# Six exponential buffers instead of three in the attention layers of a four-layer graph network

## The chip, the cores and the metric

The kernel runs on one core of a Trainium2 chip. The metric is the device time of one execution in microseconds (us), the lower the better. Before the change it is 3087.09 us, the median of three runs (3085.15, 3087.09 and 3092.65 us).

## What is computed

The input is x (3327 nodes, 256 features each) and adj (3327 x 3327, about 1% of it positive, with a positive diagonal). Four layers follow one another. Each normalises x row by row, takes the positive part, and adds the layer's result to x. Layer 0 is a top-p attention with two propagation steps. Layer 1 filters the adjacency with a tanh and multiplies it with a projection of the nodes. Layers 2 and 3 are graph attention; the change touches layers 1, 2 and 3. Cut to what matters:

```python
# layer 1
filt = tanh(adj * adj) * (adj > 0)            # the 700 largest of a row are kept
x = x + relu(filt @ (tanh(h @ W_proj + b_proj) @ W_gcn) + b_gcn)
# layers 2 and 3 (layer 2 also masks in the diagonal; layer 3 ends with elu)
Wh = h @ W
e = leaky_relu((Wh @ a[:256])[:, None] + (Wh @ a[256:])[None, :], 0.2)
alpha = softmax(where(adj > 0, e, NEG_INF), axis=1)
x = x + alpha @ Wh
```

## The kernel before

Everything is one core's program. It is written with tiles and pools; a planner in the framework then fixes, while the program is built, in which order each engine's instructions stand, and puts in the waits. Each engine works through its own list in that order, so an instruction that waits holds up everything behind it on its engine. Tiles that share a slot of memory (`slot(tag, ...)`) wait for the last use of the tile that was there.

The nodes are padded to 26 row tiles of 128. Layers 2 and 3 are two calls of `attention` (L1546 on). It takes the row tiles in seven spans: six of four tiles and a last one of two. For one span it walks over the 26 column tiles two at a time; such a step of two column tiles is called a pair here, and a span has 13 of them. What one pair costs on each engine:

- ScalarE (ACT) writes four exponentials: twice the first one, L1615, `e1 = exp(s0 + sd)`, and twice the second one, L1616, `e2 = exp(s1 + d2)` (512 elements per partition each with four tiles in the span). The larger of the two is the exponential of the leaky relu.
- VectorE (DVE) takes their maximum into e1 (L1617) and masks it with the stored signs of adj (L1618), both over 1024 elements.
- TensorE (PE) multiplies the eight blocks of e1 with Wh (L1624), 257 columns wide: 128 features in two halves and the denominator.

The places for e1 and e2 are handed out in turn by a counter:

```python
e1, e2 = exps[count[1] % 3][:, :n], exps2[count[1] % 2][:, :n]
```

Three places of e1 lie in slot e0, one place of e2 in slot e4 and one in slot e5. A place of e1 is free again when PE has multiplied it, a place of e2 when the maximum has read it.

A softmax needs a bound on each row's scores for the next span. For each of its row tiles (four, or two for the last span) DVE runs over a whole mask row, L1631 (128 x 3327, the largest dk among a row's neighbours), in the steps b = 1 to 4 of the span before; `junk` is where it writes the products that nobody reads. Then `scores_of` (L1551 on) makes small vectors of the bounds (L1554 to L1565), PE spreads them over the partitions (L1571), ACT copies them to `sb` (L1574), and ACT sets up the next `top` from `sb` (L1586), into which the next span's L1631 writes. At a span's end the denominators are inverted (L1649) and the results finished: in layer 2 with L1670, in layer 3 with L1676 to L1681 and an output DMA.

Under layer 2 the entry of layer 3 is prepared for every row tile that is finished: statistics on DVE (L131, L132), three small steps on GpSimd (POOL; L794, L795, L1414), `turned` (ACT L1420 writes hr, PE transposes it at L786, ACT copies it to ht at L787), `projected` (PE L1428, ACT L1432 and L1433), and for a whole span `spread` (PE L1445, ACT L1448, and DVE L1452 four times). These pieces are put on a list, `todo`, and one entry of it is taken per step b from 1 on.

Layer 1 (L1490 on) takes the row tiles one by one. For each it loads two halves of a column of blocks into one of three double places (two in slots e4 and e5, a third one in the pool `l1`), filters them (DVE L1501, ACT L1502), multiplies (PE L1505), and then, a few tiles behind, sums (L1483), turns and projects the entry of layer 2. It also makes the byte masks `pos` that L1631 reads (L1523) and stores them. The pool `att`, with four buffers of signs and masks, takes the memory that pool `l1` held.

Of the kernel before, what the change touches and what calls it, by code (L numbers as in the profile page):

```python
# [20 lines left out]
P = 128  # L21
N = 3327
NT = 26
# [43 lines left out]
def kernel(  # L67
# [679 lines left out]
    def layers(fast):  # L747
# [21 lines left out]
        def slot(tag, shape, name, dtype=F32):  # L769
            return big.tile(shape, dtype, tag=tag, name=name)  # L770
# [703 lines left out]
        places = [slot(f"e{4 + n}", [P, 2, HB * P], f"blk1_{n}") for n in range(2)]  # L1474
        entry2 = Entry("2", w2l, nodes(("a0", "a1"), D + 2, "wh2"), "bl", True)
        with tc.tile_pool(name="l1", bufs=2, reuse_waits="tile") as l1:
            third = l1.tile([P, 2, HB * P], F32, bufs=1, name="blk1_2")
            places = [[places[n][:, k, :] for n in range(2)] for k in range(2)] + [[third[:, n, :] for n in range(2)]]
            po_of = {}

            def summed(it):
                pre = late.tile([P, D], F32, tag="fin_a", bufs=2, name="pre")
                nc.vector.tensor_tensor(pre, po_of.pop(it), bg, ALU.add)  # L1483
                nc.vector.scalar_tensor_tensor(xn(it), pre, 0.0, xs(it), ALU.max, ALU.add)
                entry2.stats(it, xn(it))

            def projected(it):
                entry2.projected(it)
                if it in ends:
                    entry2.spread(ends.index(it))  # L1490

            for it in range(NT):
                if it % 2 == 0:
                    po2 = ps_wide()
                po = po_of[it] = po2[:, 512 * (it % 2) : 512 * (it % 2) + D]
                for hb in range(2):
                    filt = places[it % 3][hb]
                    nc.sync.dma_start(
                        filt, adj_t[it, :, hb * HB : (hb + 1) * HB, :].rearrange("p j i -> p (j i)")
                    )  # L1500
                    nc.vector.scalar_tensor_tensor(filt, filt, 0.0, filt, ALU.max, ALU.mult)  # L1501
                    nc.scalar.activation(filt, filt, AF.Tanh)  # L1502
                    for j in range(HB):
                        jc = hb * HB + j
                        nc.tensor.matmul(  # L1505
                            po, filt[:, j * P : (j + 1) * P], gw(jc), start=(jc == 0), stop=(jc == NT - 1)
                        )
                if it >= 1:
                    summed(it - 1)
                if it >= 2:  # L1510
                    entry2.turned(it - 2, xn(it - 2))
                if it == 2:
                    entry2.shifted()
                if it >= 3:
                    projected(it - 3)
                ar = slot(f"e{it % 2}", [P, NP], "adj_rows")
                r = rows_of(it)
                if r < P:
                    nc.vector.memset(ar, 0.0)
                for a, b in rows_to_load(it):  # L1520
                    nc.sync.dma_start(ar[a:b, :N], adj[it * P + a : it * P + b, :])
                pos = pos_first[:, it, :] if it in spans[0] else l1.tile([P, NP], U8, tag="pos", name="pos")
                nc.vector.tensor_scalar(  # L1523
                    pos[:, :N], ar[:, :N], 0.0, None, ALU.is_gt, ALU.add, accum_out=counts[:, it : it + 1]
                )
                nc.gpsimd.memset(pos[:, N:], 0)
                nc.sync.dma_start(pos_d[it], pos)
            summed(NT - 1)
            projected(NT - 3)
            entry2.turned(NT - 2, xn(NT - 2))  # L1530
            projected(NT - 2)
            entry2.turned(NT - 1, xn(NT - 1))
            projected(NT - 1)


        att = fast.enter_context(tc.tile_pool(name="att", bufs=1, reuse_waits="tile"))
        e0, e4, e5 = (slot(f"e{k}", [P, NP], f"places{k}") for k in (0, 4, 5))

        exps = [e0[:, 1024 * k : 1024 * (k + 1)] for k in range(3)]
        exps2 = [t[:, :1024] for t in (e4, e5)]  # L1540
        exps, exps2 = ([t.rearrange("p (t j i) -> p t j i", t=4, j=2) for t in ts] for ts in (exps, exps2))
        sbs = [e5[:, 1024 * k : 1024 * (k + 1)].rearrange("p (q m) -> p q m", q=2) for k in (1, 2)]
        junk = e4[:, 1024 : 1024 + NP // 2].bitcast(BF16)
        count = [0, 0]

        def attention(entry, finish, following=None):  # L1546
# [33 lines left out]
            for i, span in enumerate(spans):  # L1580
# [16 lines left out]
                for b, j0 in enumerate(range(0, NT, JB)):  # L1597
# [8 lines left out]
                    for j in range(0, nj, 2):  # L1606
                        jc = j0 + j
                        for q in range(2):
                            if eye and jc + q in span:
                                own = signs[:, jc + q - span[0], j + q, :]  # L1610
                                nc.vector.tensor_tensor(own, own, ident, ALU.max)
                        e1, e2 = exps[count[1] % 3][:, :n], exps2[count[1] % 2][:, :n]
                        count[1] += 1
                        for q in range(2):
                            nc.scalar.activation(e1[:, :, q, :], s0, AF.Exp, bias=sd[:, jc + q, 1:2])  # L1615
# [20 lines left out]
                            sb_next = scores_of(ahead, top)  # L1636
                    if following is not None and (i, b) == (1, 1):
                        following.shifted()
                    if b and todo:
                        for work in todo.pop(0):  # L1640
                            work()
                for k, it in enumerate(span):
                    if not eye:
# [30 lines left out]
        def finish3(it, po, rden):  # L1674
# [7 lines left out]
            for a, b in rows_to_load(it):  # L1682
                nc.sync.dma_start(out[it * P + a : it * P + b, :], o[a:b, :])

        attention(entry3, finish3)


# [82 lines left out]
```

## Time and profile before

| | |
|---|---|
| median of three runs | 3087.09 us |
| the profiled execution | 3088.28 us |
| its span, first to last instruction | 3086.4 us |
| PE busy in the span | 2806.9 us (91%) |
| DVE busy | 2405.2 us (78%) |
| ACT busy | 1932.0 us (63%) |
| last multiplication of layer 1 starts before | 2329.7 us |
| first multiplication of layer 2 | 2357.2 us |
| first multiplication of layer 3 | 2747.9 us |
| last multiplication of layer 3 | 3075.8 us |

The profile records one execution. Times on its axis run from the start of the span; the 1.9 us that the execution has over the span lie around it. L with a number is a line of the kernel. A row of a group gives the count, the busy time and the mean of one; a row of the waits gives who waited for whom, the total, the number of times and the longest; a row of a window gives the length and, for each engine, its busy time in the window. Matmuls overlap in PE, so that a PE that shows as busy may still start work late: what counts is the distance from one start to the next.

### The profile page before, as it was taken

To read this page: it belongs to the slowest core of one execution; us is meant where nothing else is said; L and a number is where in the kernel's file an instruction comes from. 1 tells how busy PE (TensorE), PEld (TensorE's weight loads), DVE (VectorE), ACT (ScalarE), POOL (GpSimd) and SP (SyncE) were. 2 spreads that over 40 slices of the span, in tenths; PEclk is the share of its full clock that TensorE was granted. 3 is DMA by queue.
4 is the path that set the end of the run, shared out by engine and by line. 5 is a ranking of instruction groups with operands and counts; after the bars stand their busy time and mean duration, and the time that the engine had idled before them with its cause. 6 is when DMAs were issued, how large, how long until landed. Compare 5 with 4: busy or idle time off the path is not lost.

```text
span 3086.4 us, 37597 instructions
## 1 busy us (share of the span) xinstructions
PE 2806.9 (91%) x13350; PEld 2274.9 (74%) x13350; DVE 2405.2 (78%) x4145; ACT 1932.0 (63%) x2583; POOL 433.7 (14%) x768
## 2 busy tenths in 40 slices
PE   7789999999999978989999988999997999979998
PEld 5467777777778756767777767888886777868887
DVE  3988688678678289998888679577766999779996
ACT  5777677678675347666677466433334667767776
POOL 0100000000001033111111115211120333210000
PEclk9889999999999999999999999999998999989999
DMA  4302312312332252222223332378870211112221
GB/s 124 95 12 76 97 48 73 97 58 68 94 98 77 79 152 78 64 59 78 75 59 92 92 111 66 136 297 324 332 254 25 65 58 57 32 49 79 76 75 36
DMA packets 186779, 302.24 MB, mean 98 GB/s; under 512 B 25116, under 2 KB 140759, under 8 KB 183255
## 3 DMA queue, kind: packets, MB, share of 16 engines
q1 hardware_dynamic: 186582, 299.75, 30.5%
q8 instruction: 107, 1.75, 0.2%
q14 instruction: 90, 0.74, 0.1%
HBM read 251.97 MB, written 47.71 MB: 97 GB/s over the span
## 4 chain that ended last, share of the span: by engine, by line
PE 22%; DVE 18%; issue 5%; ACT 4%; DMA 3%; POOL 2%; SPq 0%; ACTq 0%; DVEq 0%; POOLq 0%
PE ps_wide L1624 6%; PE ps_wide L1505 6%; DVE places L1631 3%; PE ps_out L951 3%; DVE places L1617 3%; DMA adj_rows<-in_adj 3%; DVE places L1618 2%; PE ps_acc L919 2%; ACT junk_a L1141 2%; DVE below L1146 1%; PE ps_acc L1624 1%; PE ps_out L1624 1%; DVE below L1188 1%; DVE w L1191 1%; PE ps_row L1428 1%
## 5 line engine op out<-in xcount | busy, mean ns | idle before, releaser
L1141 ACT ACTIVATE junk_a<-e,minus 128x3328 int8<-128x3328 f32 x196 | 601.8, 3070 | 4.3
L1624 PE MATMUL ps_wide<-wh,places 128*128 128x257 f32 x1872 | 452.6, 385 | 34.6 <-DVE places L1618 33.3
L1624 PEld LDWEIGHTS ps_wide<-wh,places 128*128 128x128 f32 x1872 | 356.3, 192 | 93.2 <-issue 21.8
L919 PE MATMUL ps_acc<-xf,blk 128*128 128x256 f32 x1352 | 317.7, 388 | 33.5 <-ACT xf_row L927 24.1
L919 PE MATMUL ps_acc<-h,blk 128*128 128x258 f32 x1352 | 328.6, 396 | 19.6 <-ACT xf_row L927 18.8
L919 PEld LDWEIGHTS ps_acc<-xf,blk 128*128 128x128 f32 x1352 | 256.7, 193 | 90.6 <-ACT xf_row L927 31.7
L951 PE MATMUL ps_out<-xa,wt 128*128 128x256 f32 x1352 | 314.8, 384 | 7.4 <-ACT wt L963 7.4
L951 PE MATMUL ps_out<-h,wt 128*128 128x256 f32 x1352 | 311.9, 382 | 2.6 <-ACT wt L963 2.6
L1615 ACT ACTIVATE places<-places,sd 128x512 f32<-128x512 f32 (+1 forms) x364 | 245.3, 684 | 107.4 <-PE ps_wide L1624 74.6
L919 PEld LDWEIGHTS ps_acc<-h,blk 128*128 128x128 f32 x1352 | 262.6, 198 | 67.0 <-ACT xf_row L927 23.3
L1029 DVE TENSOR_SCALAR_CACHE_REDUCE e<-ps_wide 128x1024 f32<-128x1024 f32 (+1 forms) x176 | 178.4, 1018 | 158.5 <-PE ps_wide L1055 158.0
L1505 PE MATMUL ps_wide<-gw,blk 128*128 128x256 f32 x1352 | 297.8, 380 | 0.0
L1146 DVE SCALAR_TENSOR_TENSOR below<-e,v 128x3328 f32<-128x3328 f32 x78 | 288.5, 3698 | 1.8
L951 PEld LDWEIGHTS ps_out<-xa,wt 128*128 128x128 f32 x1352 | 251.8, 192 | 43.2 <-ACT wt L963 10.3
L1505 PEld LDWEIGHTS ps_wide<-gw,blk 128*128 128x128 f32 x1352 | 257.4, 191 | 35.0
L951 PEld LDWEIGHTS ps_out<-h,wt 128*128 128x128 f32 x1352 | 250.4, 191 | 37.4 <-ACT wt L963 3.4
L1616 ACT ACTIVATE places<-places,d 128x512 f32<-128x512 f32 (+1 forms) x364 | 235.7, 682 | 42.7 <-DVE places L1617 42.3
L1617 DVE TENSOR_TENSOR places<-places,places 128x1024 f32<-128x1024 f32 (+1 forms) x182 | 209.4, 1159 | 68.0 <-ACT places L1615 67.6
L1055 PE MATMUL ps_wide<-keys,q 64*128 64x512 f32 (+1 forms) x832 | 212.9, 574 | 19.5 <-DVE e L1029 13.4
L963 ACT COPY wt<-ps_wide 128x1024 f32<-128x1024 f32 x208 | 175.0, 844 | 57.9 <-PE ps_wide L961 57.4
L1618 DVE SCALAR_TENSOR_TENSOR places<-blk_s,places 128x1024 f32<-128x1024 int8 (+1 forms) x182 | 208.9, 1156 | 2.1
L1038 ACT ACTIVATE e<-e,nm 128x3327 f32<-128x3327 f32 x44 | 134.9, 3067 | 102.7 <-DVE nm L1037 102.7
(281 smaller groups left out, 4332.3 us busy)
## 6 DMA issues: line engine op xcount, KB each, us to landing
blk<-in_adj_t SPq DMA_DIRECT2D x104, 448.0 KB, 3.4
blk<-in_adj_t SPq DMA_DIRECT2D x52, 832.0 KB, 7.5
adj_rows<-in_adj SPq DMA_DIRECT2D x25, 1663.5 KB, 8.8
blk<-in_adj_t SPq DMA_DIRECT2D x104, 384.0 KB, 3.2
blk_s<-sign_d SPq DMA_DIRECT2D x72, 256.0 KB, 2.9
blk_s<-pos_d SPq DMA_DIRECT2D x44, 416.0 KB, 3.7
pos_d<-pos SPq DMA_DIRECT2D x22, 416.0 KB, 2.7
xf_d<-xf_row SPq DMA_DIRECT2D x52, 128.0 KB, 2.1
```

Source lines behind the costliest of these rows:

```text
L919: nc.tensor.matmul(acc[:, :w], blk[:, j, :], xf(jc)[:, :w], start=(jc == 0), stop=(jc == NT - 1))
L951: nc.tensor.matmul(po, wt[:, k * P : (k + 1) * P], xa(jc)[:, :D], start=(jc == 0), stop=(jc == NT - 1))
L1029: nc.vector.tensor_scalar(e.rearrange("p (f c) -> p f c", f=2)[:, :, c0 : c0 + cw], pl.rearrange("p (f c) -> p f c", f=2)[:, :, :cw], 1.0, ...
L1055: nc.tensor.matmul(pl[:, f * 512 : f * 512 + cw], q[f * DA : (f + 1) * DA, :], kt[f * DA : (f + 1) * DA, s, c0 : c0 + cw], start=True, sto ...
L1141: nc.scalar.activation(junk, es[i], (AF.Relu, AF.Sign)[n], bias=minus[:, 0, i : i + 1], accum_out=(ga, sa)[n][:, 0, i : i + 1],)
L1146: nc.vector.scalar_tensor_tensor(below, es[i], v[:, 3, i : i + 1], es[i], ALU.is_ge, ALU.mult, accum_out=v[:, 1, i : i + 1],)
L1505: nc.tensor.matmul(po, filt[:, j * P : (j + 1) * P], gw(jc), start=(jc == 0), stop=(jc == NT - 1))
L1615: nc.scalar.activation(e1[:, :, q, :], s0, AF.Exp, bias=sd[:, jc + q, 1:2])
L1616: nc.scalar.activation(e2[:, :, q, :], s1, AF.Exp, bias=d2[:, jc + q : jc + q + 1])
L1617: nc.vector.tensor_tensor(e1, e1, e2, ALU.max)
L1618: nc.vector.scalar_tensor_tensor(e1, signs[:, :n, j : j + 2, :], 0.0, e1, ALU.is_gt, ALU.min)
L1624: nc.tensor.matmul(pos_[k], e1[:, k, q, :], wh(jc + q)[:, : D + 1], start=(jc + q == 0), stop=(eye and jc + q == NT - 1),)
```

## The change

Places. In layer 2 there are four places for e1 instead of three (the fourth is in slot e4), and still two for e2. Before layer 3 slot bl, which held layer 2's dk, is taken for three more: layer 3 has six places for e1 and three for e2. For the fourth place `junk` is made smaller: bytes instead of two-byte numbers.

Layer 1. The three double places are used in another turn (the last row tile now uses the third place, in pool l1, and the second row tile too). The byte masks get two named tiles instead of two buffers under one tag, allotted ahead of the third place, so that the third place lies 6656 bytes further on. The entry of layer 2 catches up by one row tile in the last two steps.

Layer 2. In the last span two entries of `todo` are taken per step, from step 0 on, instead of one per step from step 1 on.

```diff
--- before.py
+++ after.py
@@ -1474,6 +1474,8 @@
         places = [slot(f"e{4 + n}", [P, 2, HB * P], f"blk1_{n}") for n in range(2)]
         entry2 = Entry("2", w2l, nodes(("a0", "a1"), D + 2, "wh2"), "bl", True)
         with tc.tile_pool(name="l1", bufs=2, reuse_waits="tile") as l1:
+
+            pos_places = [l1.tile([P, NP], U8, bufs=1, name=f"pos{n}") for n in range(2)]
             third = l1.tile([P, 2, HB * P], F32, bufs=1, name="blk1_2")
             places = [[places[n][:, k, :] for n in range(2)] for k in range(2)] + [[third[:, n, :] for n in range(2)]]
             po_of = {}
@@ -1494,7 +1496,7 @@
                     po2 = ps_wide()
                 po = po_of[it] = po2[:, 512 * (it % 2) : 512 * (it % 2) + D]
                 for hb in range(2):
-                    filt = places[it % 3][hb]
+                    filt = places[(it + 1) % 3][hb]
                     nc.sync.dma_start(
                         filt, adj_t[it, :, hb * HB : (hb + 1) * HB, :].rearrange("p j i -> p (j i)")
                     )
@@ -1507,27 +1509,28 @@
                         )
                 if it >= 1:
                     summed(it - 1)
-                if it >= 2:
-                    entry2.turned(it - 2, xn(it - 2))
+
+                for k in range(it - 2 if it < NT - 1 else it - 1, it - 1 if it < NT - 2 else it):
+                    if k >= 0:
+                        entry2.turned(k, xn(k))
                 if it == 2:
                     entry2.shifted()
-                if it >= 3:
-                    projected(it - 3)
+                for k in range(it - 3 if it < NT - 1 else it - 2, it - 2 if it < NT - 2 else it - 1):
+                    if k >= 0:
+                        projected(k)
                 ar = slot(f"e{it % 2}", [P, NP], "adj_rows")
                 r = rows_of(it)
                 if r < P:
                     nc.vector.memset(ar, 0.0)
                 for a, b in rows_to_load(it):
                     nc.sync.dma_start(ar[a:b, :N], adj[it * P + a : it * P + b, :])
-                pos = pos_first[:, it, :] if it in spans[0] else l1.tile([P, NP], U8, tag="pos", name="pos")
+                pos = pos_first[:, it, :] if it in spans[0] else pos_places[it % 2]
                 nc.vector.tensor_scalar(
                     pos[:, :N], ar[:, :N], 0.0, None, ALU.is_gt, ALU.add, accum_out=counts[:, it : it + 1]
                 )
                 nc.gpsimd.memset(pos[:, N:], 0)
                 nc.sync.dma_start(pos_d[it], pos)
             summed(NT - 1)
-            projected(NT - 3)
-            entry2.turned(NT - 2, xn(NT - 2))
             projected(NT - 2)
             entry2.turned(NT - 1, xn(NT - 1))
             projected(NT - 1)
@@ -1535,12 +1538,14 @@
 
         att = fast.enter_context(tc.tile_pool(name="att", bufs=1, reuse_waits="tile"))
         e0, e4, e5 = (slot(f"e{k}", [P, NP], f"places{k}") for k in (0, 4, 5))
-
-        exps = [e0[:, 1024 * k : 1024 * (k + 1)] for k in range(3)]
-        exps2 = [t[:, :1024] for t in (e4, e5)]
-        exps, exps2 = ([t.rearrange("p (t j i) -> p t j i", t=4, j=2) for t in ts] for ts in (exps, exps2))
+        def pairs(places):
+
+            return [t[:, n : n + 1024].rearrange("p (t j i) -> p t j i", t=4, j=2) for t, n in places]
+
+        exps = pairs([(e0, 0), (e0, 1024), (e0, 2048), (e4, 2048)])
+        exps2 = pairs([(e4, 0), (e5, 0)])
         sbs = [e5[:, 1024 * k : 1024 * (k + 1)].rearrange("p (q m) -> p q m", q=2) for k in (1, 2)]
-        junk = e4[:, 1024 : 1024 + NP // 2].bitcast(BF16)
+        junk = e4[:, 1024 : 1024 + NP // 4].bitcast(U8)
         count = [0, 0]
 
         def attention(entry, finish, following=None):
@@ -1609,7 +1614,7 @@
                             if eye and jc + q in span:
                                 own = signs[:, jc + q - span[0], j + q, :]
                                 nc.vector.tensor_tensor(own, own, ident, ALU.max)
-                        e1, e2 = exps[count[1] % 3][:, :n], exps2[count[1] % 2][:, :n]
+                        e1, e2 = exps[count[1] % len(exps)][:, :n], exps2[count[1] % len(exps2)][:, :n]
                         count[1] += 1
                         for q in range(2):
                             nc.scalar.activation(e1[:, :, q, :], s0, AF.Exp, bias=sd[:, jc + q, 1:2])
@@ -1636,8 +1641,8 @@
                             sb_next = scores_of(ahead, top)
                     if following is not None and (i, b) == (1, 1):
                         following.shifted()
-                    if b and todo:
-                        for work in todo.pop(0):
+                    for _ in range(2 if ahead == [] else 1 if b else 0):
+                        for work in todo.pop(0) if todo else []:
                             work()
                 for k, it in enumerate(span):
                     if not eye:
@@ -1682,6 +1687,10 @@
             for a, b in rows_to_load(it):
                 nc.sync.dma_start(out[it * P + a : it * P + b, :], o[a:b, :])
 
+
+        bl = slot("bl", [P, NP], "places_bl")
+        exps += pairs([(bl, 0), (bl, 1024)])
+        exps2 += pairs([(bl, 2048)])
         attention(entry3, finish3)
 
 
```

## The prediction

> **What bounds the kernel now.** I first read the table of windows over layers 2 and 3, cut where the bound vectors of the next span go to PE (L1571; these points are called C, five in each layer, C0 in its first span to C4 in its fifth). Columns are the length, then busy time and count per engine, the granted clock and the DMA share.
>
> ```profile
> core 0: us, PE busy (x) PEld busy (x) DVE busy (x) ACT busy (x) POOL busy (x), PEclk, DMA share, GB/s
> 2395.80:2449.90 54.10, 49.76 (x227) 42.78 (x226) 48.48 (x59) 37.70 (x63) 19.12 (x17) 0.97 0.20 64
> 2449.90:2506.50 56.60, 52.17 (x246) 44.00 (x244) 51.56 (x68) 38.68 (x71) 24.77 (x17) 1.00 0.20 61
> 2506.50:2565.40 58.90, 53.60 (x244) 45.38 (x245) 55.35 (x71) 40.32 (x74) 21.09 (x17) 0.97 0.19 59
> 2565.40:2621.90 56.50, 52.16 (x246) 43.93 (x245) 52.40 (x70) 39.75 (x73) 18.67 (x17) 1.00 0.20 61
> ...
> 2786.20:2837.90 51.70, 49.18 (x230) 41.83 (x229) 48.12 (x53) 38.25 (x64) 0.00 (x0) 1.00 0.25 77
> 2837.90:2889.50 51.60, 49.06 (x229) 41.76 (x228) 48.02 (x53) 38.36 (x64) 0.00 (x0) 1.00 0.25 77
> 2889.50:2940.00 50.50, 48.92 (x230) 41.88 (x229) 47.94 (x53) 38.29 (x64) 0.00 (x0) 1.00 0.25 79
> 2940.00:2991.60 51.60, 49.15 (x230) 41.79 (x229) 48.09 (x53) 38.26 (x64) 0.00 (x0) 1.00 0.25 77
> ```
>
> DVE is busy 90 to 95% in each, and PE as much: neither has much to spare. DVE's idle time, 54.10 - 48.48 and so on, is 18.3 us over the four periods of layer 2 and 13.2 us over those of layer 3. That is what more places can give there at most. The waits between 2357 and 2692 us (layer 2) say what it consists of:
>
> ```profile
> ACT places L1615 <- PE ps_wide L1624: 40.0, 43, 2.3
> DVE places L1617 <- ACT places L1615: 32.0, 27, 3.3
> ACT hr L1420 <- POOL mv_a L1414: 27.4, 9, 5.1
> ```
>
> DVE waits for the first exponential, and ACT for two things: a place that PE has not freed, and POOL's statistics, behind which the exponentials stand in ACT's order. Third, the timeline at the C of 2837.85 us, for the way from there to the next span's first L1631:
>
> ```profile
> 2837.85 1.04 PE L1571 MATMUL ps_row<-ident,col 128*128 128x128 f32 x8
> 2838.73 1.05 ACT L1574 COPY places<-ps_row 128x512 f32<-128x512 f32 x2
> 2839.82 0.19 ACT L1586 COPY top<-places 128x4 f32<-128x4 f32 x1
> 2840.05 3.63 DVE L1631 CUSTOM_DVE_ANT_0 places<-blk_s,dk 128x3327 bf16<-128x3327 uint8 x1
> ```
>
> It takes 2.2 us. Last, the chain at the end of layer 1, where PE is cold:
>
> ```profile
> 2329.89 1.76 PE ps_row L1428 x8
> 2337.24 2.10 PE ps_row L1428 x4
> 2339.86 0.39 ACT ht L787
> 2340.30 2.09 PE ps_row L1428 x4
> 2343.15 0.48 ACT dk L1448
> ```
>
> **What the skill says.** "Perfetto Trace Analysis", Optimization Strategy: a gap that repeats on the engine that should be full can mean too few buffers. The trace agrees: DVE idles 0.98 us in pair after pair before the C above. "VectorE: DVE Perf Modes", the perf-mode tier table: `tensor_tensor` on float32 in SBUF has only its basic rate; the same page's formula (N+151)/0.96 gives 1224 ns for 1024, and the trace has 1218 to 1236. So DVE's work can't shrink with another place. "TensorE: Matmul & The Clock Gate", Part 1: the array runs at half clock until it has been busy some 3.4 us. Here layer 2's first multiplications are 0.43 us apart for 4.7 us, then 0.217.
>
> **The change, part by part.** Steps by distance from start to start in the trace: L1617 and L1618 1.135 each, L1631 3.54, L1624 0.434 per block (3.47 a pair), L1428 0.87 (1.72 cold), an exponential 0.61.
>
> *Places, what they remove.* In layer 3 ACT may then be six pairs ahead of PE instead of three: the 13.2 us of DVE idle time go. In layer 2 four places do it, with the built order: now ACT's first L1420 of a span stood between the two first exponentials of one pair, so that DVE starved (2.98 us at 2423.67); after the change it stands behind both of the next pair, and DVE has two pairs and an L1631 (8 us) to do while ACT waits for POOL (some 2.6 us). So the 18.3 us go too, but for 1 us.
>
> *What the new order adds.* The planner moves L1631. Now 3.5 pairs lie between the last small vector (L1565) and the next span's first L1631. After the change it follows L1565 behind one L1618 in layer 3; in layer 2 behind 4.2 us of work, behind the four L1611 (1.1 us), and twice behind nothing. But it needs L1586, and that comes 2.2 us after C plus one exponential put between (0.61), in layer 2 also an L787 (0.36). With 0.2 us from L1565 to C, DVE stands 3.0 - 1.1 = 1.9 us per span in layer 3; in layer 2 2.1 (there C is set by PE), 3.45 - 1.1 = 2.35, 3.45 and 3.45. Behind the standing L1631 wait L1617 and L1618 of the next pairs, and for those PE; PE then still has two pairs (6.9 us) to multiply, which covers all but what the sum has.
>
> *Layer 3.* Per period 48.05 busy + 1.9 = 50.0 us, four of them 200.0 against 205.4: -5.4. Cross-check along the loop: C to L1631 2.8; two L1631 and 5 steps of 1.135 to L1649: 12.8; from there 20 such steps, two L1631, 8 finishing steps of 0.4 and small ones to L1565: 33.9; to C 0.2; together 49.7. Ahead of C0 PE loses 1.66 us behind an L1631 (2759.96) that now comes four pairs later: -1.6. The span after C4 has 0.5 us of gaps on PE: -0.4. Sum -7.4.
>
> *Layer 2.* Four periods: 207.8 + 11.35 + 1 = 220.1 against 226.1: -6.0. Ahead of C0 a gap of 1.0 at 2380.6: -0.9. From C4 to the end of the sixth span PE has gaps of 5.3 us; by the new order it waits 2.4 us there for L1618 and for L1565: -3. Sum -9.9.
>
> *Layer 1's catching up.* One L1428 and two transposes (0.87 + 0.22) go ahead of the last multiplications, where PE has no idle time, so the layer ends 1.1 us later. Until now they ran in the shadow of the statistics (PE idle from 2332.2 to 2335.6). And in the new order one L1428 and the four L1445 stand behind the transpose of row tile 24, ahead of its L1428: cold 1.72 + 0.86, less 1.0 in which PE idles anyway: 1.5. POOL's L1449 no longer stands ahead of the statistics: -0.2. Sum +2.4.
>
> *Two entries of `todo` a step.* An L1428 and four L1445 (1.3 us) move ahead of layer 2's last multiplication; until now PE did them while it waited for the statistics (4.16 us idle at 2721). I see PE standing 1.4 us for POOL's third row tile, against gaps of 1.28 now. Sum +1.6.
>
> *At nothing.* The turned places of layer 1: the third place is now loaded for row tile 1, from 1998.9 us; its filter is done at 2010.0, and PE comes to it at 2011.7 (cover gone: 8 to 10 us once). Its memory now also waits for the last L972 and its store, issued at 1995.1. Signs and masks for layer 2 that lie over the third place now load after 2331 instead of 2305; first needed at 2350 (SP has nothing else queued; 8 issues of 0.5). Byte output of L1631 isn't in the trace: L1523, 3327 elements to bytes, takes 3.62, L1631 to two bytes 3.62. I take 0; the ends are -0.1 and +0.1 us each, +-4 over 44.
>
> Sum: -7.4 - 9.9 + 2.4 + 1.6 = -13.3. The profiled execution, 3088.3, becomes 3075.0; it lies 1.2 above the median, so the forecast for the median is 3073.8, 3074.
>
> **Rivals.** *The moved L1631 costs nothing*, because L1586 is done when DVE gets there. Then nearly all idle time goes: -22 in layer 2, -14 in layer 3, +4: 3055. For it: in this trace L1631 never waits for L1586 but at a layer's start (6.7 us, twice). Against it: the built order leaves at most 4 us between.
> *The idle time changes only its name*: PE stands where DVE stood, DVE waits at L1649 for PE, and only the gaps at the starts and ends go: -5.9 + 4.0: 3085. For it: PE and DVE have the same work per period (48 us in layer 3).
> *Slower*: at the moved L1631, nine periods, 11.35 + 4 x 1.9 = 19 us of new waits come, and ACT's waits for POOL and for two places of e2 stay: +19 + 4 - 5.9 = +17: 3104. It decides when less than 17 of the 31.5 us of idle time is recovered. Against it: the place of L1420.
>
> **How the numbers follow.** Forecast 0.45 (own range 3066 to 3080), no cost 0.25, name only 0.20, slower 0.10. A change below 0.3% (9 us) can't be told from none here. Faster than 3078: 0.41 + 0.25 + 0.03, about 0.69; within: 0.22; slower: 0.09. The range runs from 3054, which leaves out nearly half of the second case, to 3088, which leaves out the last: about 0.2 together. The +-4 us of the bytes lie inside.
>
> **What would show it.** Right: periods of layer 3 of about 50.0 us with DVE waiting 1.9 us for L1586 at each first L1631; ACT's wait for places (40.0 us in layer 2) falls below 15; from layer 1's last multiplication to layer 2's first some 1.3 us more than 27.7, with that last one 1.1 us later. Wrong: DVE still waits for L1615 in mid-span, or periods of 48.3 us.

## The result, and the profile after

The changed kernel takes 3079.7 us against 3089.4 us, medians of 20 executions each: 0.9969 of the time before, 95% interval 0.9962 to 0.9977, so 9.7 us less. A second series of 14 executions gave 3079.7 us again and 0.9967 (0.9958 to 0.9976). The forecast was 3074, 13.3 us less, with a range of 3054 to 3088.

The profiled execution of the changed kernel took 3074.3 us (span 3072.4), 14.0 us less span than the one before. That hits the sum of the forecast almost exactly, but it says little for it: this execution lies 5.4 us below its own median, and stage by stage the sum was wrong in nearly every term. The starts of PE's first and last multiplications of each layer cut both traces:

| stretch | forecast | before, us | after, us | difference |
|---|---|---|---|---|
| start to layer 1's first L1507 (L1505 before) | 0 | 1994.4 | 1995.6 | +1.2 |
| layer 1, first to last multiplication | +1.1 | 334.9 | 335.9 | +1.0 |
| from there to layer 2's first L1629 | +1.3 | 27.9 | 26.7 | -1.2 |
| layer 2, first to last | -8.6 | 362.4 | 359.8 | -2.6 |
| from there to layer 3's first | +0.3 | 28.3 | 26.5 | -1.8 |
| layer 3, first to the end | -7.4 | 338.4 | 327.9 | -10.5 |

(Of the tail terms of the forecast, +2.4 for layer 1 is 1.1 and 1.3; of the +1.6 at the end of layer 2, 1.3 is work that moves ahead of the last multiplication and belongs to -9.9 + 1.3 = -8.6.) The numbers of the lines have moved: L1624 is L1629 now, L1615 and L1616 are L1620 and L1621, L1617 and L1618 are L1622 and L1623, L1631 is L1636, L1571 is L1576, L1574 is L1579, L1586 is L1591, L1565 is L1570, L1649 is L1654, L1670 is L1675. The new L1616 is the old L1611, which puts the diagonal into the signs.

The table of windows of the changed kernel, cut at the points C0 to C4 of layers 2 and 3 as before: length, busy time and count per engine, granted clock, DMA share.

```profile
core 0: us, PE busy (x) PEld busy (x) DVE busy (x) ACT busy (x) POOL busy (x), PEclk, DMA share, GB/s
2395.20:2449.10 53.90, 50.69 (x237) 43.17 (x236) 49.74 (x61) 36.44 (x63) 20.03 (x17) 1.00 0.20 62
2449.10:2505.80 56.70, 53.23 (x250) 45.22 (x251) 52.85 (x69) 38.79 (x72) 23.40 (x17) 1.00 0.19 61
2505.80:2563.00 57.20, 52.88 (x237) 44.85 (x238) 52.82 (x69) 39.46 (x72) 28.09 (x17) 0.94 0.19 60
2563.00:2619.50 56.50, 52.83 (x249) 44.72 (x249) 51.87 (x69) 39.22 (x72) 25.13 (x17) 1.00 0.20 61
2781.20:2829.90 48.70, 48.49 (x229) 42.00 (x228) 46.30 (x52) 36.78 (x64) 0.00 (x0) 1.00 0.22 68
2829.90:2879.10 49.20, 48.66 (x229) 42.03 (x228) 47.67 (x53) 36.90 (x64) 0.00 (x0) 1.00 0.25 81
2879.10:2927.80 48.70, 48.68 (x229) 41.95 (x228) 46.74 (x53) 36.71 (x64) 0.00 (x0) 1.00 0.26 81
2927.80:2976.60 48.80, 48.59 (x230) 42.05 (x229) 47.32 (x53) 36.81 (x64) 0.00 (x0) 1.00 0.26 82
```

In layer 3 PE is now busy 48.49 to 48.68 us of 48.7 to 49.2: PE has become the bound, full to 1%. In layer 2 nothing like it happened. Its four periods add up to 224.3 us against 226.1, and DVE still idles 17.0 us in them (224.3 - 207.3), against 18.3. In a second profiled execution of the same kernel (`r_after`, below) they add up to 226.8 us, so that even the 1.8 us are not sure.

The waits of the changed kernel between 2357 and 2690 us, layer 2 (time, times, longest):

```profile
ACT hr L1420 <- POOL mv_a L1414: 29.0, 12, 5.5
...
ACT places L1620 <- PE ps_wide L1629: 20.8, 26, 1.4
DVE places L1622 <- ACT places L1620: 15.9, 10, 2.9
...
DVE places L1636 <- ACT top L1591: 9.3, 5, 2.8
```

ACT's wait for a place that PE frees has halved, from 40.0 to 20.8 us, and with it DVE's wait for the first exponential, from 32.0 to 15.9. But ACT waits as long as ever for POOL's statistics (27.4 before), and a wait that did not exist has come, at L1636.

The timeline of the changed kernel at C1 of layer 3, the way that the forecast followed:

```profile
2829.92 1.04 PE L1576 MATMUL ps_row<-ident,col 128*128 128x128 f32 x8
...
2830.56 1.07 ACT L1579 COPY places<-ps_row 128x512 f32<-128x512 f32 x2 [9.91 <-PE ps_row L1576]
...
2831.51 0.73 ACT L1620 ACTIVATE places<-places,sd 128x512 f32<-128x512 f32 x1
2832.14 0.19 ACT L1591 COPY top<-places 128x4 f32<-128x4 f32 x1
...
2832.36 3.63 DVE L1636 CUSTOM_DVE_ANT_0 places<-blk_s,dk 128x3327 uint8<-128x3327 uint8 x1 [1.53 <-ACT top L1591]
```

DVE stands 1.53 us at the moved sweep (the L1631 of the kernel before, called a sweep from here on), for L1591 and the one exponential ahead of it, where the forecast had 1.9; in the other three periods it stands 4.4, 2.0 and 1.5 us. What these stands cost is another question: below.

I then added up DVE's idle time in the four periods of a layer by the instruction that ended it (gaps over 0.06 us between neighbours in DVE's list):

| kernel, layer | at L1622, for an exponential | at L1636, for L1591 | at L1616, for a sign transfer |
|---|---|---|---|
| before, layer 2 | 17.8 | 0 | 0 |
| changed, layer 2 | 8.1 | 7.4 | 1.5 |
| before, layer 3 | 12.4 | 0 | 0 |
| changed, layer 3 | 0 | 9.4 | 0 |

So layer 2 asks why the first column did not empty, and layer 3 why 9.4 us in the second cost next to nothing. The theory: in layer 2, ACT stands for POOL's statistics with the exponentials queued behind it, longer than any four places can bridge; in layer 3 the places alone are the gain. The rivals: the stand at L1591 is what holds layer 2, or four places are too few, or the gain comes from the rest of the change.

### The profile page after: what moved, and what is told of

It is laid out like the page before. It is cut to its first block, busy times and chain, and to the rows that moved or that the text cites. A ratio compares the mean times of both kernels' runs of the same rounds, so it can differ in the third digit from the quotient of the medians.

```text
span 3072.4 us, 37544 instructions
## 1 busy us (share of the span) xinstructions
PE 2808.1 (91%) x13350; PEld 2278.8 (74%) x13350; DVE 2396.1 (78%) x4145; ACT 1922.3 (63%) x2583; POOL 455.8 (15%) x768
## 5 line engine op out<-in xcount | busy, mean ns | idle before, releaser
L1629 PE MATMUL ps_wide<-wh,places 128*128 128x257 f32 x1560 | 377.2, 385 | 27.6 <-DVE places L1623 19.7
L1629 PEld LDWEIGHTS ps_wide<-wh,places 128*128 128x128 f32 x1560 | 297.9, 193 | 74.4 <-issue 22.8
L1507 PE MATMUL ps_wide<-gw,blk 128*128 128x256 f32 x1352 | 299.2, 381 | 0.0
L1507 PEld LDWEIGHTS ps_wide<-gw,blk 128*128 128x128 f32 x1352 | 258.1, 191 | 35.4
L1620 ACT ACTIVATE places<-places,sd 128x512 f32<-128x512 f32 (+1 forms) x304 | 206.0, 686 | 34.3 <-PE ps_wide L1629 25.8
L1621 ACT ACTIVATE places<-places,d 128x512 f32<-128x512 f32 (+1 forms) x304 | 201.2, 685 | 27.5 <-DVE places L1622 25.8
L961 PE MATMUL ps_wide<-ident,e 128*128 128x128 f32 x1144 | 157.6, 277 | 36.8 <-DVE e L1202 21.4
L1191 DVE MAX8 w<-below 128x8 f32<-128x3328 f32 x52 | 188.3, 3622 | 0.3
```

The costliest lines, as they stand in the source:

```text
L1191: nc.vector.max(w9[:, i, 1:9], below)
L1507: nc.tensor.matmul(po, filt[:, j * P : (j + 1) * P], gw(jc), start=(jc == 0), stop=(jc == NT - 1))
L1621: nc.scalar.activation(e2[:, :, q, :], s1, AF.Exp, bias=d2[:, jc + q : jc + q + 1])
L1629: nc.tensor.matmul(pos_[k], e1[:, k, q, :], wh(jc + q)[:, : D + 1], start=(jc + q == 0), stop=(eye and jc + q == NT - 1),)
```

## The experiments

**The places alone** (`e_places`, and once more as `r_places`). Layer 1 and the list are those of the kernel before:

```diff
-                    for _ in range(2 if ahead == [] else 1 if b else 0):
-                        for work in todo.pop(0) if todo else []:
+                    if b and todo:
+                        for work in todo.pop(0):
                             work()
```

and in layer 1 the old order of places, L1420 and L1428.

> The places alone: four, six and three places as in the changed kernel; layer 1 and the list of extra work of layer 2's last span as in the kernel before. If the places bring the gain of layer 3: from layer 3's first multiplication to the end 328 us (changed kernel 327.9, before 338.4), layer 2 from its first to its last multiplication about 360 (changed 359.8, before 362.4), and the two ways between the layers as before, 27.9 and 28.3 us (changed 26.7 and 26.5). Time about 3078, 2 to 3 us above the changed kernel. If the catching up of layer 1 and the list are what gains: 3086 or more.

> The places alone once more, the base of the next three. If its first time, 3071.1 from four executions, is its level: 3070 to 3075, 5 to 9 us below the changed kernel's 3079.7. If that was the luck of four executions: 3077 to 3080, and the rest of the change costs nothing.

Measured: 3071.1 us, ratio 0.9941 (0.9924 to 0.9957), and 3075.8 us, 0.9952 (0.9940 to 0.9965). The ten executions of both together have a median of 3074.0. Layer 3 takes 327.0 and 326.8 us and the ways between the layers 27.9 to 28.4, as expected; layer 2 takes 357.1 and 356.3, where 360 was expected. The places are the whole gain, and the rest of the change takes some of it back: 6 us by the medians, though the intervals of the ratios overlap. In layer 2 they gain nothing in the four periods (227.0 and 227.1 us, before 226.1): the 5 to 6 us lie ahead of C0 (36.6 and 37.3 us, before 38.5) and behind C4 (93.4 and 91.9 us, before 97.8). With other places the planner also builds another order, in which the sweeps have moved. No kernel here has the places in the old order, so that "the places" means both.

**The rest alone** (`e_rest`): the changed kernel with three and two places in both layers.

```diff
-        exps = pairs([(e0, 0), (e0, 1024), (e0, 2048), (e4, 2048)])
+        exps = pairs([(e0, 0), (e0, 1024), (e0, 2048)])
...
-        bl = slot("bl", [P, NP], "places_bl")
-        exps += pairs([(bl, 0), (bl, 1024)])
-        exps2 += pairs([(bl, 2048)])
```

> The rest alone: layer 1 and the list as in the changed kernel, but three places for first exponentials and two for second ones in both layers. If the places bring the gain: layer 3 is back at 338 us, the four periods of layer 2 at some 226 us, only the ways between the layers stay short (26.7 and 26.5): 3086 us, 3 below the kernel before. If the rest is what gains: 3080.

Measured: 3092.3 us, 1.0008 (1.0001 to 1.0015), where 3086 was expected. Layer 3 is back at 339.3 us and layer 2 at 364.4. The ways between the layers are short as expected (25.8 and 26.2), but layer 2 itself is 2.0 us longer than before. The rest gains nothing; it costs a little.

**Which half of the rest** (`e_layer1`, `e_todo`, and the changed kernel again as `r_after`). `e_layer1` keeps the new layer 1 and has the old list (the diff of the list above, alone); `e_todo` keeps the new list and has the old layer 1.

> The changed kernel once more, beside the kernels that take a part of it out. The places alone gave 3071.1 against a kernel before of 3089.8, the changed kernel 3079.7 against 3089.4, though the two profiled executions have spans of 3072.0 and 3072.4. If the rest of the change costs time that one profiled execution does not show: 3078 to 3081 here as well, with its executions spread over some 20 us. If the difference was one of chips: 3071 to 3074.

> The places and the new layer 1 (turned places, catching up), with the old list of layer 2's last span. If layer 1 is what costs the 8 us between the places alone and the changed kernel: 3079 to 3081. If the list costs them: 3071 to 3073. By the profiled executions the new layer 1 gains about 1 us on the way to layer 2 (26.7 against 27.9).

> The places and two entries of the list a step in layer 2's last span, with the old layer 1. If the list costs the 8 us: 3079 to 3081. If layer 1 costs them: 3070 to 3073. By the profiled executions the list gains 1.9 us on the way to layer 3 (26.5 against 28.4) and puts 1.3 us more ahead of layer 2's last multiplication.

Measured: the changed kernel 3079.7 (0.9967), with the old list 3072.6 (0.9952, 0.9938 to 0.9965), with the old layer 1 3075.4 (0.9960, 0.9947 to 0.9974). The medians point at the list, but five executions each don't part the two. The traces do: from the C that belongs to layer 2's last span to the C that belongs to layer 3's first one it takes 71.7, 69.9 and 71.8 us with four places and the old list (`e_places`, `r_places`, `e_layer1`), and 74.9, 74.9 and 77.8 with the new one (changed kernel, `e_todo`, `r_after`): 3 to 8 us more. (With three places and the old list it took 76.4 us before: here the fourth place had gained, and the list takes it back.) The timeline of PE in `r_after` shows it:

```profile
2697.99 0.38 PE L786 MATMUL ps_row<-ident,hr 128*128 128x128 f32 x2
2698.21 1.04 PE L1428 MATMUL ps_row<-w3l,ht 128*128 128x258 f32 x4
2702.70 0.69 PE L786 MATMUL ps_row<-ident,hr 128*128 128x128 f32 x2 [3.45 <-ACT ht L787]
2703.18 1.92 PE L1629 MATMUL ps_wide<-wh,places 128*128 128x257 f32 x4
2704.89 1.93 PE L1428 MATMUL ps_row<-w3l,ht 128*128 128x258 f32 x4
```

Two entries a step bring the transposes of row tiles so close that PE stands 3.45 us in the middle of the multiplications, since POOL has not made the statistics: in this stretch ACT waits 13.9 us for them, with the old list 5.3. And then PE runs at half its rate: four L1629 take 1.7 us from start to start and four L1428 as long, against 0.87 otherwise. In the profiled execution of the changed kernel the same stand was not followed by that (four L1629 in 0.87 us at 2699.10), which is 2.6 us of the difference between the two executions; why not stays open. Without the list there is no such gap: PE of `e_places` passes its pairs and transposes without a stand.

```profile
2704.90 0.38 PE L786 MATMUL ps_row<-ident,hr 128*128 128x128 f32 x2
2705.11 1.04 PE L1428 MATMUL ps_row<-w3l,ht 128*128 128x258 f32 x4
2705.99 3.63 PE L1629 MATMUL ps_wide<-wh,places 128*128 128x257 f32 x16
```

**No wait for L1591** (`e_notop`). The first values of `top`, all overwritten, come from another tile:

```diff
-                nc.scalar.copy(top, sb[:, 1, :4])
+                nc.scalar.copy(top, entry.tops[:, :, 0])
```

> The changed kernel, but the copy that gives top its first values (L1591) reads entry.tops instead of sb, so that the sweeps of L1636 do not wait for it. The copied values are all overwritten, except that columns of a short last span are not used. If the wait for L1591 (12.6 us over layer 2) is what holds layer 2: its periods fall from 56.5 to about 54.3, and those of layer 3 from 48.8 to 48.0; 3067 us. If the statistics on POOL hold layer 2, its periods stay within 0.7 us of 56.5 and the time within 4 us of the changed kernel; the freed sweeps may also be put ahead of the small vectors, which then come later.

Measured: 3089.8 us, 1.0003 (0.9994 to 1.0011): the whole gain is lost. Both expectations had a part of it. Three of the four periods of layer 2 do shorten: 54.6, 54.9, 53.6 and 56.3, together 219.3 against 224.3. But the planner, free to do so, now puts the sweeps wherever they fit first, and that is ahead of the small vectors on which the next span waits. DVE's timeline in `e_notop`:

```profile
2451.68 0.16 DVE L1567 TENSOR_SCALAR top<-top 128x4 f32<-128x4 f32 x1
2451.75 3.62 DVE L1636 CUSTOM_DVE_ANT_0 places<-blk_s,dk 128x3327 uint8<-128x3327 uint8 x1
2455.30 0.15 DVE L1569 TENSOR_TENSOR col<-sd,top 128x4 f32<-128x4 f32 x1
```

L1569 has nothing else to wait for and comes 3.6 us behind L1567. At the starts of the layers the way to the first multiplication grows by 6.5 and 5.4 us, the period after C4 of layer 2 from 37.2 to 44.4, and layer 3's periods to 49.1 to 49.8. So the edit does not price the wait cleanly; it suggests that the wait had also been holding the sweeps in their place.

**No wait for the statistics** (`e_nostat`). In layer 2, L1420 goes without its scale and bias:

```diff
-                nc.scalar.activation(hr, src, AF.Relu, bias=mv[:, 0:1], scale=mv[:, 1:2])
+                nc.scalar.activation(hr, src, AF.Relu, **(dict(bias=mv[:, 0:1], scale=mv[:, 1:2]) if self.eye else {}))
```

> The changed kernel, but in layer 2 L1420 applies no scale and bias, so that layer 3's input is not normalised; POOL still makes the statistics, but nothing in layer 2 waits for them. If the statistics hold layer 2: its periods fall from 56.5 to about 52.5 (DVE busy 51.9, PE 52.8), the four together from 224.3 to about 211, the end of layer 2 comes 2 us sooner too (no statistics on the way to layer 3), and the time is about 3062. If the wait for L1591 or too few places hold it: periods within 1 us of those of the changed kernel, 3077.

Measured: 3055.0 us, 0.9889 (0.9872 to 0.9905). Layer 2 takes 345.7 us, 14.0 less than in the changed kernel, and the way to layer 3 22.0, 4.5 less. Its four periods in the table of windows:

```profile
2396.10:2447.00 50.90, 50.02 (x238) 43.46 (x237) 48.80 (x61) 36.61 (x63) 29.42 (x17) 1.00 0.19 60
2447.00:2501.60 54.60, 52.76 (x251) 45.30 (x252) 52.67 (x69) 38.38 (x72) 30.05 (x17) 1.00 0.20 64
2501.60:2557.00 55.40, 50.40 (x239) 43.24 (x240) 52.61 (x69) 39.19 (x72) 30.34 (x17) 1.00 0.20 62
2557.00:2611.60 54.60, 52.19 (x247) 44.52 (x248) 51.89 (x69) 39.16 (x72) 30.30 (x17) 1.00 0.21 64
```

Together 215.5 against 224.3, where 211 was expected. DVE's idle time is 9.5 us, and of the three columns above the first is empty: 0 at L1622, 8.0 at L1636, 1.6 at L1616. The order of DVE's instructions in this kernel is that of the changed one in these periods. On ACT L1420 stands earlier, and in the later periods some exponentials and L787 stand elsewhere too, so that the wait is not the only thing that differs. Both causes are there, and the one goes without the other: 8.1 us of idle time went with the wait for the statistics, 7.4 to 8.0 are the moved sweep.

**Three places in layer 2** (`e_l2three`) and **four in layer 3** (`e_l3as2`), both from the places alone. In the first the fourth place (e4, 2048) is added only ahead of layer 3; in the second the three lines with `bl` are gone.

> The places alone, but layer 2 keeps three places for first exponentials; layer 3 has its six and three. If the fourth place gains as little in layer 2 as the profile of the changed kernel says (2.6 us of 362): layer 2 from its first to its last multiplication about 361 us (with four places 357, before 362.4), the four periods about 226 us, layer 3 unchanged at 327; time 3 to 5 us above the places alone. If the fourth place is worth what was forecast: 367 and 10 us more.

> The places alone, but layer 3 has layer 2's four places and two of the second kind, instead of six and three. If four are enough where no statistics stand among the exponentials: periods of layer 3 within 0.4 us of 48.8 and 327 to 329 us in all. If six are needed to bridge the way back over ACT and the waits at L1636: periods of 50 to 51 us (with three and two 51.4) and 333 to 336 us.

Measured: 3077.0 us (0.9958, 0.9946 to 0.9971) and 3073.9 us (0.9951, 0.9938 to 0.9964); neither can be told from the places alone in time (0.9952 beside them). In the traces, layer 2 with three places takes 360.6 us, 3.6 to 4.4 more than with four. But none of that lies in the periods, which are 224.6 us with three and 227.0 with four; it lies ahead of C0 (38.2 us with three) and behind C4 (97.9). Layer 3 with four places, from the table of windows:

```profile
2780.80:2830.00 49.20, 48.72 (x230) 42.07 (x229) 46.72 (x52) 37.88 (x64) 0.00 (x0) 1.00 0.22 69
2830.00:2879.50 49.50, 48.59 (x229) 41.99 (x228) 47.73 (x53) 38.05 (x64) 0.00 (x0) 1.00 0.26 82
```

0.3 us more per period than with six. PE is as full. Where nothing interrupts ACT four places are enough; the fifth and sixth, and the third for the second exponential, carry 1.3 us in four periods.

**The factor later** (`e_scale`): a version meant to keep the normalisation and lose the wait. The factor is positive, so Relu((x - mean) f) is f Relu(x - mean), and f can wait until behind the projection. From the places alone:

```diff
-                nc.gpsimd.tensor_scalar(mv[:, 0:1], mv[:, 0:1], mv[:, 1:2], -1.0, ALU.mult, ALU.mult)
+                nc.vector.tensor_scalar(mv[:, 0:1], mv[:, 0:1], -1.0, None, ALU.mult)
...
-                nc.scalar.activation(hr, src, AF.Relu, bias=mv[:, 0:1], scale=mv[:, 1:2])
+                nc.scalar.activation(hr, src, AF.Relu, bias=mv[:, 0:1])
...
-                nc.scalar.copy(self.sd[:, it, :], ps[:, D : D + 2])
-                nc.scalar.copy(wh[:, :D], ps[:, :D])
+                nc.scalar.activation(self.sd[:, it, :], ps[:, D : D + 2], AF.Copy, scale=self.mv[it][:, 1:2])
+                nc.scalar.activation(wh[:, :D], ps[:, :D], AF.Copy, scale=self.mv.pop(it)[:, 1:2])
```

with six buffers for `mv_a` instead of three.

> The places alone, and the factor of the normalisation applied later: L1420 takes Relu(x - mean), with -mean from DVE, and the two copies L1432 and L1433 multiply by the factor, which POOL makes in the meantime; the function is the same, since the factor is positive. ACT then waits for POOL two pairs later than now. If the wait of L1420 for POOL, with the exponentials behind it, is what holds layer 2: its periods fall from 54 to 58 us to 51 to 54.6 as in the kernel without the normalisation, the ways between the layers from 27.9 and 28.4 to about 26 and 23, and the time is 3052 to 3058. If POOL is as late at L1432 and L1433: within 4 us of the places alone, 3071.

Measured: 3063.0 us, 0.9920 (0.9906 to 0.9933), some 5 us short of the hope. ACT's wait for POOL at L1420 is gone, and no wait for POOL came at L1432 or L1433. Layer 2's periods are 51.1, 54.6, 55.6 and 55.9 us. Layer 1 is left in 23.4 instead of 27.9 us, but layer 2 only in 27.3.

**And the copy earlier** (`e_scale_top0`): L1591 of that kernel reads the row that is ready first.

```diff
-                nc.scalar.copy(top, sb[:, 1, :4])
+                nc.scalar.copy(top, sb[:, 0, :4])
```

> The kernel with the later factor (3063.0), and in it L1591 copies from the first of the two bound rows instead of the second, so that it follows L1579 at once and the first exponential of the next span stands behind it. DVE's wait for L1591 falls by one copy of 0.5 to 0.6 us or one exponential of 0.6 us for each span. If this wait is what is left: periods of layer 3 from 48.8 to about 48.2, those of layer 2 by 0.6 to 1 us; time 3056 to 3059. If DVE's time is used up by PE's anyhow (PE 48.6 of 48.8 us): 3061 to 3064.

Measured: 3056.7 us, 0.9896 (0.9882 to 0.9910). With it the four periods of layer 2 and two of layer 3 look so:

```profile
2395.80:2446.30 50.50, 49.70 (x235) 42.95 (x233) 48.60 (x63) 37.18 (x63) 23.77 (x13) 1.00 0.18 55
2446.30:2500.70 54.40, 52.11 (x246) 44.44 (x246) 52.86 (x73) 39.92 (x72) 23.01 (x13) 1.00 0.21 63
2500.70:2555.50 54.80, 53.03 (x251) 45.26 (x252) 52.80 (x73) 40.39 (x72) 21.18 (x13) 1.00 0.21 63
2555.50:2609.50 54.00, 50.60 (x232) 43.01 (x233) 52.17 (x73) 40.10 (x72) 18.61 (x13) 0.97 0.20 64
2764.80:2813.50 48.70, 48.65 (x229) 42.03 (x228) 46.39 (x52) 36.77 (x64) 0.00 (x0) 1.00 0.22 66
2813.50:2862.20 48.70, 48.64 (x229) 42.03 (x228) 47.42 (x53) 36.77 (x64) 0.00 (x0) 1.00 0.27 82
```

In layer 2 the periods add up to 213.7 us, 3.5 less than without this edit, and DVE stands 5.7 us at L1636 instead of 7.0. In layer 3 DVE's stands fall too, from 9.5 to 7.5 us, but the four periods lose only 0.6 us together and are 48.7 us each, where PE is busy 48.6: there the second expectation held. This kernel is the fastest here that computes the whole function (`e_nostat` leaves the normalisation out), 33 us below the kernel before and 23 us below the changed one, if the medians are compared; the ratio against the kernel before is the measured one.

## Why the prediction was right in its range, and wrong in its terms

**Layer 3: -7.4 forecast, -10.5 measured.** The start was right to the digit (-1.6 ahead of C0), and behind C4 came +1.0 instead of -0.4, most of it after the last multiplication. The periods were not right: 50.0 forecast, 48.7 to 49.2 measured, so that C0 to C4 went from 205.4 to 195.4 us, -10.0 instead of -5.4. The step that failed is "Per period 48.05 busy + 1.9 = 50.0 us", and in it the first term. The stand was right in sum: DVE idles 7.4 us in the four windows, 1.85 per period (the rest of the 9.4 us lies ahead of C0). But the busy time of 48.05 us contained waiting: two DVE instructions without a wait between them overlap (starts 1.135 us apart, 1.218 long), one behind a wait does not. The trace after has 47.0 us for the same instructions. Of the 208 instructions in the four periods 170 overlapped with the next one before and 204 do now; 34 times 0.083 us is 2.8 of the 4.1 us.

PE, with 48.6 us of its own work, now sets the period, and the stands lie behind enough finished pairs that PE hardly feels them: in the period ahead of C1 DVE stood 4.4 us, and PE was idle 0.2 us. The margin is small. L1576 starts 0.2 to 0.7 us behind the end of L1570 at C1 to C4, and 0.07 us where PE has nothing else to do. The cross-check along DVE's loop gave 49.7 because it took the loop to run through DVE alone, and priced the way from C to the sweep at 2.8 us, where it takes 2.44.

**Layer 2: -8.6 forecast, -2.6 measured.** The step that failed is "after the change it stands behind both of the next pair, and DVE has two pairs and an L1631 (8 us) to do while ACT waits for POOL (some 2.6 us)". The order was as described. The wait was not 2.6 us. These are lines of the changed kernel's timeline around the first L1420 of a span, of POOL, DVE and ACT:

```profile
2470.76 1.10 POOL L794 TENSOR_SCALAR mv_a<-mv_a 128x1 f32<-128x1 f32 x1 [7.48 <-DVE mv_a L132]
...
2473.52 1.79 POOL L1414 TENSOR_SCALAR mv_a<-mv_a 128x1 f32<-128x1 f32 x1
...
2475.17 3.61 DVE L1636 CUSTOM_DVE_ANT_0 places<-blk_s,dk 128x3327 uint8<-128x3327 uint8 x1
2475.34 0.60 ACT L1420 ACTIVATE hr<-xs,mv_a 128x256 f32<-128x256 f32 x1 [4.28 <-POOL mv_a L1414]
2475.38 3.48 POOL L794 TENSOR_SCALAR mv_a<-mv_a 128x1 f32<-128x1 f32 x1
...
2479.61 0.78 POOL L1414 TENSOR_SCALAR mv_a<-mv_a 128x1 f32<-128x1 f32 x1
...
2480.43 0.60 ACT L1420 ACTIVATE hr<-xs,mv_a 128x256 f32<-128x256 f32 x1 [0.81 <-POOL mv_a L1414]
...
2482.28 1.23 DVE L1622 TENSOR_TENSOR places<-places,places 128x1024 f32<-128x1024 f32 x1 [1.93 <-ACT places L1620]
```

ACT waits 4.28 us for the first row tile's statistics and 0.81 for the second, with the exponentials behind both, and then DVE stands 1.93 us for one of them. Places do not help here, since ACT is not waiting for one. The 18.3 us did not go "but for 1 us": 8.1 us stayed at L1622. Of the 11.35 us of new stands at L1631, 7.4 came, and 1.5 more at L1616, where DVE now comes ahead of a transfer of signs. `e_nostat` shows the first of these terms by itself.

By stretch, the four periods gave -1.8 us instead of -6.0 (and +0.7 in `r_after`), the way to C0 -1.6 instead of -0.9, and what lies behind C4 +0.7 instead of -1.7. In size that is nearer to the rival that had 0.20, in which only the gaps at the starts and ends go, and the places alone did just that. Its mechanism did not come: DVE waits for PE at the new L1654 for 1.7 us, as before, and the idle time went to the sweeps instead.

**The ends of the layers: +1.3 and +0.3 forecast, -1.2 and -1.8 measured.** The order came as forecast: one L1428 and the L1445 stand ahead of row tile 24's L1428. The chain of the changed kernel at the end of layer 1:

```profile
2335.15 0.22 POOL mv_a L794
...
2335.46 0.27 POOL mv_a L1414
2335.76 0.61 ACT hr L1420
...
2337.10 1.72 PE ps_row L1428 x4
2338.82 0.85 PE ps_row L1445 x4
2339.68 1.77 PE ps_row L1428 x4
...
2342.40 1.15 PE ps_row L1428 x4
```

In the kernel before, the same POOL instruction and the first L1420 were:

```profile
2333.83 1.10 POOL L1414 TENSOR_SCALAR mv_a<-mv_a 128x1 f32<-128x1 f32 x1
...
2334.97 0.60 ACT L1420 ACTIVATE hr<-xs,mv_a 128x256 f32<-128x256 f32 x1 [2.03 <-POOL mv_a L1414]
```

The steps that failed are the 1.5 us for these two pieces and, beside them, "POOL's L1449 no longer stands ahead of the statistics: -0.2". The first L1420 comes 4.2 us after the last multiplication (2331.5), where it came 5.7 us after it (2329.3), and the second after 5.1 instead of 7.0 us. POOL's statistics are shorter now that DVE's L1452 do not run beside them: the first row tile's L1414 takes 0.27 us instead of 1.10, the second one's L795 0.57 instead of 1.03. So the two pieces fill time in which PE had waited, and row tile 24's L1428 starts 7.9 us after the last multiplication, as before. And PE is at full rate sooner: row tile 25's four L1428 are 0.22 us apart, not 0.43, and from their start to the last L1445 it takes 1.4 us instead of 2.3. That is most of the -1.2.

At the end of layer 2 the first L1420 comes after 3.4 instead of 5.2 us; the three POOL instructions ahead of it take 1.05 us instead of 2.33. But there the price of two entries a step lies inside the layer (3.45 us in the last span), and the forecast of 1.4 us for that stand was too small by 2.

**At nothing** was right where it can be seen: L1636 to bytes takes 3.62 us, as to two bytes; layer 1 takes 334.9 and 335.9 us from first to last multiplication. Its spread over the kernels here (332.5 to 338.5 us with the old layer 1, 333.1 to 337.2 with the new one) hides such terms, and also the 1.1 us that were forecast for the work that moves into it.

**The signs named ahead.** DVE's stand at L1591 is there in every span, as said. Periods of 50.0 us, ACT's wait for places below 15 us in layer 2 (20.8) and a longer way out of layer 1 are all refuted, and the sign that was named for "wrong", a DVE that still waits for the first exponential in mid-span, is there in layer 2. The other one, periods of 48.3 us, is nearer to layer 3's 48.7 to 49.2 than 50.0 is. The total held because +6.0 in layer 2 stood against -3.1 in layer 3 and -4.6 at the two ends: that it came within the range is in good part luck.

Three slips in the working are small beside this: the "nine periods" of new waits are eight, the +1.6 for the list comes to 1.4 as it is worked out (1.3 + 1.4 - 1.28), and the way out of layer 1 was 27.9 us, not 27.7.

The median of the changed kernel lies 5.9 us above the forecast for it (3073.8). `r_after` was profiled in an execution with a span of 3079.0: there layer 1 begins 4.3 us later than in the first profile, and layer 2 takes 364.8 us instead of 359.8, part of it after the stand that the list brings. What makes executions differ by 7 us ahead of layer 1 (its first multiplication lies between 1992.9 and 1999.8 us in these traces, with the same program up to there) stays open. That the rest of the change costs 6 us is supported by medians and by the 3 to 8 us in the last span; that it is the list and not layer 1 is shown in the traces only.

## What to carry to other kernels

Before more buffers are given to a queue, read what its producer waits for: places help only where the producer waits for a place. Here ACT had two reasons to be late, and the one that it shares its order with, a short instruction that waits for a slow engine, held layer 2 once the other was gone. Moving the slow factor behind a linear step took another 11 us (3074.0 to 3063.0), where the places had taken 15. And check which engine is full before a stand is charged to the end, and do not take busy time for work: DVE's fell from 48.0 to 47.0 us a period here when its waits went.

## What was not expected of the hardware

POOL's small instructions on one column can take as long as the DVE instruction that runs beside them. Over the changed kernel L794 on `mv_a` takes 213 ns at best (224 in the median) and 3483 ns at worst, L795 542 to 5475, L1414 260 to 4403. Of the long ones in layer 2's four periods L794 and L1414 end 0.05 to 0.14 us behind the end of an L1622, L1623 or L1636, L795 some 0.42 us behind it, and all those over 3 us lie under an L1636 (3.62 us). The Trainium skill, "SBUF — State Buffer", section "SBUF: two separate sides", says why: VectorE and GpSimd share a pair of ports, and an instruction of VectorE with two inputs in SBUF takes it, against one of GpSimd that reads SBUF, as "an exclusive lock, not a bandwidth split". The trace agrees in when they end, and the effect is large: the 48 instructions of the statistics between C0 and C4 of layer 2 take 57.5 us in the kernel before, 70.1 in the changed one (64.7 in `r_after`) and 84.1 in `e_nostat`. Most of the difference is in those that run beside a sweep: 7 of the 48 before, with 22.4 us, then 11 with 36.9 us, then 15 with 45.8 us. DVE's busy time in the four periods was nearly the same before and after (207.8 and 207.3 us). That is why the same chain of three POOL instructions, which needs 1.1 us when DVE is elsewhere, could not be priced from its median. The change moved sweeps over the statistics, and the wait that it had to shorten, L1420's, stayed at 29.0 us (27.4 before).
